# Finishing the last pair tile by tile: plain products for its output stage and its last two layers, buffers in places of x, and its heads placed closer together in the queue

## The chip, the cores and the metric

The kernel runs on one core of one Trainium2 chip. The metric is the device time of one execution in microseconds (us); lower is better. Engines are named as in the profile: PE (TensorE, matrix products; PEld is its weight load), DVE (VectorE), ACT (ScalarE), POOL (GpSimd) and SP (SyncE, which issues nearly all DMA transfers of this kernel).

## The reference, cut to what matters

The input x has 128 graphs of 64 nodes with 512 features. One adjacency matrix of 64x64 serves all graphs. Four layers follow one another; each adds its result to x and normalizes every row (layernorm without scale).

```python
x = _layernorm(x + L0(x))   # deg * (x Wi^T + b) + adj (x Wj^T)
x = _layernorm(x + L1(x))   # 4 attention heads + elu, output attention + elu, FFN, layernorm
x = _layernorm(x + L2(x))   # one graph attention head, product with W2
x = _layernorm(x + L3(x))   # the same with W3

def L1(x):
    h = elu(heads(x))                      # 4 heads of 512 -> 2048 features per row
    o = elu(attention(h @ W_out))          # one output head
    y = relu(o @ w1 + b1) @ w2 + b2 + o
    return layernorm(y) * gamma + beta

def L2(x):                                 # L3 alike
    Wh = x @ W
    logits = leaky_relu(Wh @ a_src + (Wh @ a_dst)^T, 0.2), masked by adj
    return softmax(logits) @ Wh
```

Everything is float32. The attention of one graph mixes only that graph's 64 rows, so two graphs of 64 rows make a tile of 128 rows that depends on no other tile.

## The kernel before, in words

The 8192 rows are cut into 32 pairs (NP), each of T = 2 tiles of P = 128 rows. A pair passes through five stages, each a Python generator: `stage_first` (layer 0), `stage_scores` (attention of the four heads, and the attention product with x), `stage_heads` (the heads' weight products, one generator for all pairs), `stage_project` (product with W_out into the tile `who`, in two halves q = 0 and 1, and the output attention's dots), and `stage_late`. That last one runs `stage_out` (output attention, elu, FFN, norms) and then `stage_gat` twice (layers 2 and 3). The FFN's second product and the products with W2 and W3 are Strassen-like: `strassen` and `seven` compute both tiles of a pair at once by 7 products in place of 8. Each product goes into one of two PSUM tiles (stx and sty in the profile), sums of operands are made on POOL, and DVE adds each partial result. Normalization of the first tile follows product 4, that of the second product 6. The weights of these products come as parts from DRAM (ws, wk) for each pair. hidp is already a plain product.

Two orders matter. First, a queue `queue` decides in which order the generators are asked for their next steps: each `yield n` puts the stage n units later. A turn is TURN = 107.0 units; pair p's stages start at fixed positions such as TURN * (p + 1.42) for its late stage. `seven` yields a gap between products (TURN / H / 8 in the heads); `stage_project` pauses TURN / 2 - 14.0 between its halves. At most UNITS = 3 products of seven are open in that order. Second, each step gets its number in this order as its rank. The planner (`Plan.order`) then simulates the engines with its own costs: on each engine the ready step of the lowest rank goes next. The result is the fixed instruction order of each engine. `soon()` lowers a step's rank; `together()` keeps calls in one step.

Buffers have tags with a number of places: x has 5 (one per pair in flight), who and o 1 each, A, rows, ys, s2 and s3 2 each, hT 4 (one per head), ax 1, PSUM 8 banks. A step that opens a tile waits until a place is free; the planner gives places within a reach of 160 steps (NEAR). `rows` loads one or two 512-element rows, broadcast over 128 partitions, into the rows tag.

At the end of the program the last pair but one (NP - 2) and the last (NP - 1) have start positions, paces and rests of their own:

```python
at, pace, rest = {NP - 2: (1.6, 1.0, 10.0), NP - 1: (1.3, 0.6, 0.0)}.get(
    p, (1.42, 1.0, 5.0)
)
start(TURN * (p + at), 10 * p, stage_late(p, pace, rest))
```

`pace` multiplies the late stage's yields, `rest` is added ahead of each of layers 2 and 3.

Of the kernel before, what the change touches and what calls it, by code (L numbers as in the profile page):

```python
# [12 lines left out]
FP = mybir.dt.float32  # L13
# [326 lines left out]
def gnn_stack_kernel(  # L340
# [347 lines left out]
    def moments(x, name):  # L688

        stats = small.tile([P, 6], FP, tag="stats", name=f"st_{name}")  # L690
        mv = small.tile([P, 2], FP, tag="mv", name=f"mv_{name}")
        nc.vector.bn_stats(stats, x)
        nc.vector.bn_aggr(mv, stats)
        rstd = small.tile([P, 1], FP, tag="rstd", name=f"rs_{name}")
        nc.gpsimd.tensor_scalar(rstd, mv[:, 1:2], EPS, None, ALU.add)
        nc.gpsimd.tensor_tensor(rstd, rstd, mhalf, ALU.pow)
        return mv[:, 0:1], rstd

    def normalize(x, name):

        mean, rstd = moments(x, name)
        shift = small.tile([P, 1], FP, tag="shift", name=f"sh_{name}")
        nc.vector.scalar_tensor_tensor(shift, mean, -1.0, rstd, ALU.mult, ALU.mult)
        nc.scalar.activation(x, x, AF.Identity, bias=shift, scale=rstd)
# [52 lines left out]
                nc.scalar.copy(aT[ts(b, N), :, s, :], pt[ts(s, N), :, ts(b, N)])  # L757
        return aT

    def attention(f, alpha, mask, fill, has, name):  # L760

        bc3 = [P, T, N]
        ps = psum.tile([P, T, P], FP, tag="b", name=f"bc_{name}")
        with nc.together():
            for t in range(T):
                nc.tensor.transpose(ps[:, t, :], f[:, 1, t : t + 1].to_broadcast([P, P]), ident)
        e = unit.tile(bc3, FP, tag="e1", bufs=2, name=f"e_{name}")
        with nc.soon():
            for b in range(2):
                nc.vector.tensor_tensor(  # L770
                    e[ts(b, N), :, :], ps[ts(b, N), :, ts(b, N)],
                    f[ts(b, N), 0, :].unsqueeze(2).to_broadcast([N, T, N]), ALU.add,
                )
# [19 lines left out]
        pt = psum.tile([P, P], FP, tag="b", name=f"pt_{name}")  # L793
        nc.tensor.transpose(pt, e.rearrange("p t j -> p (t j)"), ident)
        return pt

    def elu(dst, ps):

# [141 lines left out]
    def stage_heads():  # L940

        for i in range(NP * H):
            p, h = divmod(i, H)
            while p not in ys:
                yield 1.0
            y, t1, t2 = ys[p][h // 2]
            y, t1, t2 = y[:, :, h % 2, :, :], t1[:, :, h % 2, :], t2[:, :, h % 2, :]
            Y = lambda k, t: y[:, 2 * k : 2 * k + 2, t, :]
            w = w_h[h]
            hT = unit.tile([P, KC, T, P], FP, tag="hT", bufs=H, name=f"hT_{p}_{h}")  # L950

# [12 lines left out]
            def t4():  # L964
                nc.gpsimd.tensor_tensor(Y(1, 0), Y(1, 0), t2, ALU.subtract)

            yield from seven(
                product, lambda i, j: hT[:, 2 * i : 2 * i + 2, j, :], [2, P], f"h_{p}_{h}",
                TURN / H / 8, True,
                t4,  # L970
                lambda i: elu_of(hT[:, 2 * i : 2 * i + 2, :, :], f"{p}_{h}_{i}"),
            )
            hTs[p, h] = hT
            if h == H - 1:
                ys.pop(p)

    def stage_project(p):

        who = unit.tile([P, T, D], FP, tag="who", name=f"who_{p}")
        for q in range(H // 2):  # L980
            while (p, 2 * q + 1) not in hTs:
                yield 1.0
            h = [hTs.pop((p, 2 * q + k)) for k in range(2)]
            A = lambda k, t: h[k][:, :, t, :]
            nc.gpsimd.tensor_tensor(A(0, 1), A(0, 1), A(1, 1), ALU.add)
            yield from strassen(
                A, part_from(f"wo{q}", p), sums(A, KC, nc.gpsimd), who, KC, f"o_{p}_{q}", 3.0,
                fresh=q == 0,
            )
            if q == 0:  # L990
                yield TURN / 2 - 14.0
        r = rows([a_out[ts(s, D)] for s in range(2)], f"1o_{p}")
        yield 4.0
        f = small.tile([P, 2, T], FP, tag="f1", name=f"f_1o_{p}")
        dots(lambda s, t: f[:, s, t : t + 1], who, r, f"1o_{p}")
        outs[p] = (who, f)
        yield 0.0

    def stage_out(p):

        while p not in outs:
            yield 1.0
        x = xs[p]
# [9 lines left out]
        yield 2.0  # L1013
        o = unit.tile([P, T, D], FP, tag="o", name=f"o_{p}")
        oT = unit.tile([P, KC, T * P], FP, tag="A", bufs=NA, name=f"oT_{p}")

# [36 lines left out]
            yield 6.0  # L1053
        gamma_sb = rows([gamma], f"gamma_{p}")[:, 0, :]

        def norms(t):
            ot, xt = o[:, t, :], x[:, t, :]
            mean, rstd = moments(ot, f"1i_{p}_{t}")
            ps = psum.tile([P, D], FP, tag="b", name=f"ng_{p}_{t}")
            with nc.soon():  # L1060
                nc.vector.scalar_tensor_tensor(ps, ot, mean, gamma_sb, ALU.subtract, ALU.mult)
                nc.vector.scalar_tensor_tensor(xt, ps, rstd, xt, ALU.mult, ALU.add)
            normalize(xt, f"1_{p}_{t}")

        A = lambda k, t: hid[:, k, t, :, :]
        nc.gpsimd.tensor_tensor(A(0, 1), A(0, 1), A(1, 1), ALU.add)
        yield from strassen(
            A, part_from("w2", p, D // 2), sums(A, KC // 2, nc.gpsimd), o, KC // 2, f"y_{p}", 1.8,
            whole=norms,
        )  # L1070
        yield 4.0

    def stage_gat(p, name):
# [48 lines left out]
        if name == "3":  # L1122
            xs.pop(p)

    def stage_late(p, pace, rest):

        for later in stage_out(p):
            yield later * pace
        for name in ("2", "3"):
            yield rest  # L1130
            for later in stage_gat(p, name):
                yield later * pace


    queue = []

    def start(at, order, stage):
        heapq.heappush(queue, (at, order, stage))

    for p in range(NP):  # L1140
        if p < AHEAD:
            start(TURN * (0.2 * p - 1.2), 10 * p + 4, stage_first(p))
        else:
            start(TURN * (p - 1.1), 10 * p + 4, stage_first(p))
        start(TURN * (p - 0.5), 10 * p + 3, stage_scores(p))
        start(TURN * (p + 0.6), 10 * p + 2, stage_project(p))

        at, pace, rest = {NP - 2: (1.6, 1.0, 10.0), NP - 1: (1.3, 0.6, 0.0)}.get(
            p, (1.42, 1.0, 5.0)
        )  # L1150
        start(TURN * (p + at), 10 * p, stage_late(p, pace, rest))
    start(0.0, 10 * NP, stage_heads())
    start(-1.15 * TURN, 0, score_weights(
        [head_rows(w) for w in w_h], a_h, "h", lambda h: head_sums(w_h[h])
# [67 lines left out]
```

## Time and profile before

| | |
|---|---|
| median of 3 runs | 3366.57 us (3366.22 to 3369.87) |
| the profiled execution | 3368.96 us, its span 3367.2 us, mean granted clock of PE 0.989 |
| PE busy over the span | 98%; PEld 86%, DVE 73%, ACT 40%, POOL 51% |
| last product of the last pair's projection starts | 3257.45 us |
| last write of x by ACT | 3363.1 us |
| DMA over the span | 720 MB, 214 GB/s |

All instructions have the line L306 of a helper, so they are told apart by their tiles. In the names, ws_W is a part of W2 or W3, ws_w one of w2, ws_wo one of W_out; stx and sty with no suffix belong to layers 2 and 3 (and layer 0), with _o to the projection, with _y to the FFN, with _h to the heads. bc and pt are an attention's two transposes (with _1o those of the output attention), op its product, gp the attention product of layers 2 and 3. j and f are the dots with score rows. A float32 matmul is shown as two instructions, called halves below. Buffer numbers are left out, so the trace doesn't say which pair an instruction belongs to; that follows from order and dependences.

### The profile page before, as it was taken

The numbers are of one execution on the slowest core, as the hardware profiler recorded it, in microseconds if no ns is written. First come the engines' busy times: TensorE is split into PE (matmuls) and PEld (weight loads), VectorE is DVE, ScalarE is ACT, GpSimd is POOL, SyncE is SP. The second block draws the span as 40 slices with busy tenths as digits, with TensorE's granted clock in tenths as the row PEclk, the third lists the DMA queues.
The fourth block names the chain that finished last, engine by engine and source line by source line (L and its number), as shares of the span: only waits on it lengthen the run. The fifth ranks groups of instructions, "written<-read, shape, count | busy, mean of one in ns | idle before, by whom it ended". The sixth has DMA issues, their size and how long they took to land. (4 is left out here: it accounts for less than half of the span.)

```text
span 3367.2 us, 59757 instructions
## 1 busy us (share of the span) xinstructions
PE 3287.4 (98%) x21300; PEld 2901.8 (86%) x21300; DVE 2448.8 (73%) x5696; ACT 1354.8 (40%) x3180; POOL 1719.0 (51%) x1866
## 2 busy tenths in 40 slices
PE   8899999999999999999999999999999999999986
PEld 4788988888988988988888988988988888989974
DVE  6757777777777777777777777777767777777755
ACT  1344444444444343444443443443444433443432
POOL 6854455554455554455554455554455554555433
PEclk9899999999999999999999999999999999999997
DMA  8766667666666666666666666666666666666653
GB/s 285 260 218 207 206 215 223 215 222 217 207 205 230 217 218 220 213 207 222 216 217 224 205 214 217 216 216 229 202 216 214 221 211 225 198 222 210 205 162 112
DMA packets 302501, 720.43 MB, mean 214 GB/s; under 512 B 32848, under 2 KB 42112, under 8 KB 302208
## 3 DMA queue, kind: packets, MB, share of 16 engines
q1 hardware_dynamic: 302208, 716.63, 65.0%
q8 instruction: 171, 2.80, 0.3%
q14 instruction: 122, 1.00, 0.1%
HBM read 683.18 MB, written 33.32 MB: 213 GB/s over the span
## 5 line engine op out<-in xcount | busy, mean ns | idle before, releaser
L306 DVE CUSTOM_DVE_ANT_0 j<-x,rows 128x512 bf16<-128x512 f32 x736 | 616.7, 838 | 67.8 <-ACT x L306 35.7
L306 PE MATMUL stx_h<-ys,wh 128*128 128x128 f32 x3072 | 405.9, 276 | 0.9 <-ACT hT L306 0.5
L306 PEld LDWEIGHTS stx_h<-ys,wh 128*128 128x128 f32 x3072 | 387.1, 192 | 21.1 <-issue 9.2
L306 ACT COPY hT<-stx_h 128x256 f32<-128x256 f32 x384 | 143.0, 372 | 506.6 <-PE stx_h L306 497.2
L306 POOL TENSOR_SCALAR rs<-mv 128x1 f32<-128x1 f32 x256 | 85.4, 334 | 402.1 <-DVE mv L306 389.9
L306 ACT ACTIVATE x<-x,sh,rs 128x512 f32<-128x512 f32 x256 | 207.5, 814 | 201.1 <-DVE sh L306 199.2
L306 PE MATMUL sty_h<-ys,wh 128*128 128x128 f32 x2048 | 276.0, 278 | 0.6 <-ACT hT L306 0.6
L306 DVE TENSOR_TENSOR x<-stx,x 128x256 f32<-128x256 f32 x368 | 153.5, 419 | 158.0 <-PE stx L306 156.9
L306 PEld LDWEIGHTS sty_h<-ys,wh 128*128 128x128 f32 x2048 | 253.1, 193 | 13.3 <-issue 5.7
L306 PE MATMUL sty_o<-ws_wo,hT 128*128 128x256 f32 x1024 | 244.2, 381 | 1.7 <-DMA ws_wo<-d_wo 1.7
L306 PE MATMUL stx_o<-ws_wo_T,s_o 128*128 128x256 f32 x1024 | 244.6, 382 | 0.5 <-DVE who L306 0.3
L306 POOL TENSOR_TENSOR ys<-ys,t 128x256 f32<-128x256 f32 x128 | 113.2, 887 | 254.3 <-PE sty_h L306 254.2
L306 PE MATMUL hidp<-oT,w 128*128 128x256 f32 x1024 | 231.5, 379 | 0.7 <-ACT oT L306 0.7
L306 DVE TENSOR_TENSOR hT<-sty_h,hT 128x256 f32<-128x256 f32 x256 | 107.9, 421 | 165.9 <-PE sty_h L306 138.9
L306 PEld LDWEIGHTS hidp<-oT,w 128*128 128x128 f32 x1024 | 191.7, 190 | 25.2 <-ACT oT L306 0.9
L306 PEld LDWEIGHTS sty_o<-ws_wo,hT 128*128 128x128 f32 x1024 | 188.7, 190 | 26.6 <-issue 1.9
L306 PEld LDWEIGHTS stx_o<-ws_wo_T,s_o 128*128 128x128 f32 x1024 | 185.9, 190 | 25.6 <-DVE who L306 2.6
L306 ACT ACTIVATE elu<-hT 128x512 f32<-128x512 f32 x256 | 153.4, 601 | 102.8 <-DVE hT L306 91.4
L306 DVE SCALAR_TENSOR_TENSOR hT<-elu,hT 128x512 f32<-128x512 f32 x256 | 173.0, 682 | 28.7 <-ACT elu L306 26.0
L306 DVE BATCH_NORM_STATS2 st<-x 128x6 f32<-128x512 f32 x256 | 176.4, 689 | 5.5
L306 POOL TENSOR_TENSOR rs<-rs,mhalf 128x1 f32<-128x1 f32 x256 | 153.8, 601 | 21.3
L306 ACT COPY ys<-yp 128x512 f32<-128x512 f32 x256 | 131.3, 605 | 78.9 <-PE yp L306 73.2
(187 smaller groups left out, 7730.6 us busy)
## 6 DMA issues: line engine op xcount, KB each, us to landing
ws_wo_T<-d_wo_T SPq DMA_DIRECT2D x256, 512.0 KB, 3.9
ws_wo<-d_wo SPq DMA_DIRECT2D x192, 512.0 KB, 3.5
ws_W_T<-d_W_T SPq DMA_DIRECT2D x256, 256.0 KB, 3.6
rows<-d_h SPq DMA_DIRECT2D x240, 256.0 KB, 4.2
ws_w_T<-d_w_T SPq DMA_DIRECT2D x112, 512.0 KB, 4.2
ws_W<-d_W SPq DMA_DIRECT2D x192, 256.0 KB, 3.6
ws_w<-d_w SPq DMA_DIRECT2D x84, 512.0 KB, 4.2
ws_w_T<-d_w_T SPq DMA_DIRECT2D x128, 256.0 KB, 4.4
```

The costliest lines, as they stand in the source:

```text
L306: getattr(getattr(self.tc.nc, s.engine), name)(*map(real, args), **{k: real(v) for k, v in kw.items()})
```

## The change

Only the last pair and the one before it are scheduled or computed differently. For pair NP - 1, `stage_late` is replaced by `stage_last` (loads the whole of w2, W2, W3 and rows for b2 and gamma once, does the output attention for both tiles, loads the score rows of layers 2 and 3) and one `stage_tile` for each tile, which does elu, FFN, norms and both layers for 128 rows with plain products of 128x512. The heads' gaps and the projection's pause of that pair are multiplied by 0.6. Its `who` and `o` take places of the x tag, the whole weights those of ax and ys, the rows of b2 and gamma one of hT. The late stage of pair NP - 2 starts at 2.0 in place of 1.6, with pace 0.8 and no rest. `attention` gets T as an argument, `norms` becomes a function of its own, and the attention part of `stage_out` becomes `out_attention`.

```diff
-                TURN / H / 8, True,
+                TURN / H / 8 * haste(p), True,
...
-        who = unit.tile([P, T, D], FP, tag="who", name=f"who_{p}")
+        pool, tag = (unit, "who") if p < NP - 1 else (xp, "x")
+        who = pool.tile([P, T, D], FP, tag=tag, name=f"who_{p}")
...
-                yield TURN / 2 - 14.0
+                yield (TURN / 2 - 14.0) * haste(p)
...
+    def stage_last(p):
+        raw = {}
+        for name, src, tag, bufs in (("w2", w2, "ax", 1), ("W2", W2, "ys", 2), ("W3", W3, "ys", 2)):
+            raw[name] = unit.tile([P, KC, D], FP, tag=tag, bufs=bufs, name=f"{name}_last")
+            nc.sync.dma_start(out=raw[name], in_=src.rearrange("(c p) o -> p c o", p=P))
+        r = unit.tile([P, 2, D], FP, tag="hT", bufs=H, name="rows_last")
+        for i, src in enumerate((b2, gamma)):
+            nc.sync.dma_start(out=r[:, i, :], in_=src.partition_broadcast(P))
+        who, aT = yield from out_attention(p)
+        o = xp.tile([P, T, D], FP, tag="x", name=f"o_{p}")
+        shared.update(raw=raw, rows=r, who=who, aT=aT, o=o)
+        yield 2.0
+        for name in ("2", "3"):
+            shared[name] = rows([score[name][s, :] for s in range(2)], f"{name}_{p}")
+            yield 2.0
+
+    def stage_tile(p, t):
+        while "3" not in shared:
+            yield 1.0
+        x, o, r, raw = xs[p][:, t, :], shared["o"][:, t, :], shared["rows"], shared["raw"]
+        who, aT = shared["who"], shared["aT"]
+        def plain(lhsT, w, into, name):
+            ps = psum.tile([P, D], FP, tag="b", name=name)
+            for k in range(KC):
+                nc.tensor.matmul(ps, lhsT=lhsT(k), rhs=w[:, k, :], start=(k == 0), stop=(k == KC - 1))
+            nc.vector.tensor_tensor(into, ps, into, ALU.add)
+        ps = psum.tile([P, D], FP, tag="b", name=f"op_{p}_{t}")
+        with nc.together():
+            for b in range(2):
+                nc.tensor.matmul(
+                    ps[ts(b, N), :], lhsT=aT[ts(t, N), b, :], rhs=who[ts(t, N), b, :],
+                    start=True, stop=True)
+        elu(o, ps)
+        yield 3.0
+        both = unit.tile([P, 2, KC, P], FP, tag="A", bufs=NA, name=f"oT_{p}_{t}")
+        oT, hid = both[:, 0, :, :], both[:, 1, :, :]
...
+        nc.scalar.copy(oT, ps)
+        nc.gpsimd.tensor_tensor(o, o, r[:, 0, :], ALU.add)
+        yield 3.0
...
+        yield 4.0
+        plain(lambda k: hid[:, k, :], raw["w2"], o, f"yp_{p}_{t}")
+        norms(o, x, r[:, 1, :], f"{p}_{t}")
+        yield 8.0
+        for name in ("2", "3"):
+            f = small.tile([P, 2], FP, tag="f1", name=f"f_{name}_{p}_{t}")
...
+            pt = yield from attention(
+                f.unsqueeze(2), 0.2, mask2, never.to_broadcast([P, N]), has, f"{name}_{p}_{t}", 1)
+            aT = unit.tile([P, P], FP, tag="s3", bufs=2, name=f"aT_{name}_{p}_{t}")
+            nc.gpsimd.memset(aT, 0.0)
+            for b in range(2):
+                nc.scalar.copy(aT[ts(b, N), ts(b, N)], pt[:, ts(b, N)])
+            yield 2.0
+            gT = unit.tile([P, KC, P], FP, tag="s2", bufs=2, name=f"gT{name}_{p}_{t}")
+            ps = psum.tile([P, KC, P], FP, tag="b", name=f"gp{name}_{p}_{t}")
...
+            nc.scalar.copy(gT, ps)
+            yield 3.0
+            plain(lambda k: gT[:, k, :], raw[f"W{name}"], x, f"z{name}_{p}_{t}")
+            normalize(x, f"{name}_{p}_{t}")
+            yield 6.0
+        nc.sync.dma_start(out=out[ts(p * T + t, P), :], in_=x)
...
+    haste = lambda p: 0.6 if p == NP - 1 else 1.0
...
-        at, pace, rest = {NP - 2: (1.6, 1.0, 10.0), NP - 1: (1.3, 0.6, 0.0)}.get(
+        at, pace, rest = {NP - 2: (2.0, 0.8, 0.0), NP - 1: (1.3, 0.6, 0.0)}.get(
             p, (1.42, 1.0, 5.0)
         )
-        start(TURN * (p + at), 10 * p, stage_late(p, pace, rest))
+        if p < NP - 1:
+            start(TURN * (p + at), 10 * p, stage_late(p, pace, rest))
+        else:
+            start(TURN * (p + at), 10 * p, stage_last(p))
+            for t in range(T):
+                start(TURN * (p + at), 10 * p + 1 + t, stage_tile(p, t))
```

More of the change, by code (lines that the diff above doesn't have):

```diff
@@ L758, in attention_heads, with attention @@
         return aT
-    def attention(f, alpha, mask, fill, has, name):
+    def attention(f, alpha, mask, fill, has, name, T=T):
         bc3 = [P, T, N]
@@ L791, in attention, with norms @@
         yield 8.0
-        pt = psum.tile([P, P], FP, tag="b", name=f"pt_{name}")
+        pt = psum.tile([T * N, P], FP, tag="b", name=f"pt_{name}")
         nc.tensor.transpose(pt, e.rearrange("p t j -> p (t j)"), ident)
         return pt
+    def norms(o, x, gamma_sb, name):
+        mean, rstd = moments(o, f"1i_{name}")
+        ps = psum.tile([P, D], FP, tag="b", name=f"ng_{name}")
+        with nc.soon():
+            nc.vector.scalar_tensor_tensor(ps, o, mean, gamma_sb, ALU.subtract, ALU.mult)
+            nc.vector.scalar_tensor_tensor(x, ps, rstd, x, ALU.mult, ALU.add)
+        normalize(x, f"1_{name}")
     def elu(dst, ps):
@@ L997, in stage_project, with out_attention @@
         yield 0.0
-    def stage_out(p):
+    def out_attention(p):
         while p not in outs:
             yield 1.0
-        x = xs[p]
         who, f = outs.pop(p)
@@ L1013, in stage_out @@
         yield 2.0
+        return who, aT
+    def stage_out(p):
+        x = xs[p]
+        who, aT = yield from out_attention(p)
         o = unit.tile([P, T, D], FP, tag="o", name=f"o_{p}")
@@ L1054, in stage_out @@
         gamma_sb = rows([gamma], f"gamma_{p}")[:, 0, :]
[L1056 to L1063, printed above, removed]
         A = lambda k, t: hid[:, k, t, :, :]
@@ L1068, in stage_out @@
             A, part_from("w2", p, D // 2), sums(A, KC // 2, nc.gpsimd), o, KC // 2, f"y_{p}", 1.8,
-            whole=norms,
+            whole=lambda t: norms(o[:, t, :], x[:, t, :], gamma_sb, f"{p}_{t}"),
         )
@@ L1123, in stage_gat @@
             xs.pop(p)
+    shared = {}
+    def stage_last(p):
[6 more added lines that the diff above has]
+            nc.sync.dma_start(out=r[:, i, :], in_=src.partition_broadcast(P))
+        who, aT = yield from out_attention(p)
+        o = xp.tile([P, T, D], FP, tag="x", name=f"o_{p}")
[4 more added lines that the diff above has]
+            yield 2.0
@@ new lines, in stage_tile @@
+    def stage_tile(p, t):
[7 more added lines that the diff above has]
+                nc.tensor.matmul(
+                    ps, lhsT=lhsT(k), rhs=w[:, k, :], start=(k == 0), stop=(k == KC - 1)
+                )
+            nc.vector.tensor_tensor(into, ps, into, ALU.add)
+        ps = psum.tile([P, D], FP, tag="b", name=f"op_{p}_{t}")
+        with nc.together():
+            for b in range(2):
+                nc.tensor.matmul(
+                    ps[ts(b, N), :], lhsT=aT[ts(t, N), b, :], rhs=who[ts(t, N), b, :],
+                    start=True, stop=True,
+                )
+        elu(o, ps)
+        yield 3.0
+        both = unit.tile([P, 2, KC, P], FP, tag="A", bufs=NA, name=f"oT_{p}_{t}")
+        oT, hid = both[:, 0, :, :], both[:, 1, :, :]
+        ps = psum.tile([P, KC, P], FP, tag="b", name=f"oTp_{p}_{t}")
+        with nc.together():
+            for k in range(KC):
+                nc.tensor.transpose(ps[:, k, :], o[:, ts(k, P)], ident)
+        nc.scalar.copy(oT, ps)
+        nc.gpsimd.tensor_tensor(o, o, r[:, 0, :], ALU.add)
+        yield 3.0
+        ps = psum.tile([P, KC, P], FP, tag="b", name=f"hidp_{p}_{t}")
+        for c in range(KC):
+            with nc.together():
+                for k in range(KC):
+                    nc.tensor.matmul(
+                        ps[:, c, :], lhsT=w1_sb[:, k, ts(c, P)], rhs=oT[:, k, :],
+                        start=(k == 0), stop=(k == KC - 1),
+                    )
+        for c in range(KC):
+            nc.scalar.activation(
+                hid[:, c, :], ps[:, c, :], AF.Relu, bias=b1_sb[:, c : c + 1]
+            )
+        yield 4.0
[4 more added lines that the diff above has]
+            f = small.tile([P, 2], FP, tag="f1", name=f"f_{name}_{p}_{t}")
+            for s in range(2):
+                junk = unit.tile([P, D], BF, tag="junk", name=f"j_{name}_{p}_{t}_{s}")
+                nc.vector.tensor_tensor_reduce(
+                    junk, x, shared[name][:, s, :], 1.0, 0.0, ALU.mult, ALU.add,
+                    accum_out=f[:, s : s + 1],
+                )
+            yield 2.0
+            pt = yield from attention(
+                f.unsqueeze(2), 0.2, mask2, never.to_broadcast([P, N]), has, f"{name}_{p}_{t}", 1
+            )
+            aT = unit.tile([P, P], FP, tag="s3", bufs=2, name=f"aT_{name}_{p}_{t}")
+            nc.gpsimd.memset(aT, 0.0)
+            for b in range(2):
+                nc.scalar.copy(aT[ts(b, N), ts(b, N)], pt[:, ts(b, N)])
+            yield 2.0
+            gT = unit.tile([P, KC, P], FP, tag="s2", bufs=2, name=f"gT{name}_{p}_{t}")
+            ps = psum.tile([P, KC, P], FP, tag="b", name=f"gp{name}_{p}_{t}")
+            with nc.together():
+                for c in range(KC):
+                    nc.tensor.matmul(
+                        ps[:, c, :], lhsT=x[:, ts(c, P)], rhs=aT, start=True, stop=True
+                    )
+            nc.scalar.copy(gT, ps)
[4 more added lines that the diff above has]
+        nc.sync.dma_start(out=out[ts(p * T + t, P), :], in_=x)
```

## The prediction, made before the result was known

> **What bounds the kernel now.** I read the page's slices first, then the busy time by stretch, then TensorE's timeline and the chain of waits at the end. The slices (tenths busy, then granted clock) show a full TensorE everywhere but at both ends:
>
> ```profile
> PE   8899999999999999999999999999999999999986
> PEclk9899999999999999999999999999999999999997
> ```
>
> By stretch the columns are: stretch, length, then busy us (and instructions) of PE, PEld, DVE, ACT, POOL, then clock, DMA share, GB/s:
>
> ```profile
> 3000.00:3100.00 100.00, 100.00 (x655) 89.15 (x654) 71.57 (x173) 40.48 (x93) 49.40 (x56) 1.00 0.64 208
> 3200.00:3261.70 61.70, 59.27 (x326) 51.89 (x324) 35.98 (x84) 20.25 (x50) 23.62 (x31) 1.00 0.59 187
> ...
> 3279.40:3312.30 32.90, 26.18 (x117) 20.17 (x116) 22.33 (x55) 10.88 (x24) 13.93 (x20) 0.90 0.52 159
> 3312.30:3339.70 27.40, 17.17 (x67) 13.35 (x67) 13.39 (x36) 4.98 (x13) 7.70 (x12) 0.79 0.41 132
> 3339.70:3367.20 27.50, 13.49 (x50) 10.36 (x50) 10.44 (x30) 4.89 (x14) 4.43 (x9) 0.69 0.15 51
> 3261.70:3367.20 105.50, 65.89 (x267) 50.88 (x267) 57.42 (x156) 25.62 (x69) 29.62 (x44) 0.77 0.34 106
> ```
>
> Until 3259 TensorE sets the pace: only less work ahead of that point could help. From 3261.7, where DVE has added the last product of the last pair (31) into `who`, to the end, 105.5 us, no engine is full: PE 62%, DVE 54%. That tail is a chain of latencies; in it lie pair 30's layers 2 and 3 and all of pair 31 behind `who`. Its milestones on TensorE's timeline (start, length, instruction, idle before):
>
> ```profile
> 3257.45 1.99 PE L306 MATMUL stx_o<-ws_wo_T,hT 128*128 128x256 f32 x8 [0.17 <-DVE who L306]
> ...
> 3279.40 1.09 PE L306 MATMUL op<-who,aT_1o 64*64 64x512 f32 x8
> ...
> 3285.71 3.72 PE L306 MATMUL hidp<-oT,w 128*128 128x256 f32 x16 [0.68 <-ACT oT L306]
> ...
> 3319.18 3.79 PE L306 MATMUL gp<-aTg,x 128*128 128x128 f32 x16 [0.74 <-ACT aTg L306]
> ...
> 3347.70 3.78 PE L306 MATMUL gp<-aTg,x 128*128 128x128 f32 x16 [1.22 <-ACT aTg L306]
> ```
>
> In pair 31: 17.7 us from `who` to its output attention's product (op), 32.9 to its normalized x (3312.3), 27.4 for layer 2 (to 3339.7), 24.2 for layer 3 (to 3363.9), 3.3 to the end; sum 105.5. The chain of waits names a weight load and seven products in a fixed order:
>
> ```profile
> 3326.55 3.67 DMA ws_W_T<-d_W_T
> ...
> 3357.23 2.13 issue
> ```
>
> **What the Trainium skill says.** "TensorE: Matmul & The Clock Gate", section "What's actually happening": the array runs at half clock after an idle window of about 3.4 us, and at full clock after as long a busy one. The trace agrees: 16 halves of gp take 1.95 us at 3228.5, inside the full stretch, and 3.78 at 3347.7 in the tail. "VectorE: DVE Perf Modes", section "The TRN2 errata": an fp32 tensor_tensor of N elements takes (N+151)/0.96 ns. The trace agrees (290 ns for N = 128 against 292 measured; 691 for 512 against 692), so I use it for N = 64, which no row shows: 224 ns, an estimate.
>
> **The change, part by part** (positions below are in the queue's own turns; a step that is ready and has the lower position goes first; they are no times).
>
> 1. *Where `who` of pair 31 ends.* The heads' gap times 0.6 ends their positions 0.4 turn earlier (31.6, not 32.0); the pause in `stage_project` falls from 39.5 to 23.7, so the second half of the projection lies at 32.04 to 32.27, not 32.19 to 32.42. Pair 30's late stage goes from 31.6 to 32.0. TensorE is full there, so only the order counts: what is moved behind `who` brings it forward. Pair 30's output stage holds on PE: op 1.0, oTp 0.9, hidp 32 halves by 0.216 = 6.9, y 7 products by 0.865 = 6.05, small transposes 0.3; 15.2 in all, all ahead of 3257.5 now. Its Strassen product (32.25 to 32.38) surely goes behind, the rest partly, as ready steps fill gaps. Bounds 0 and 15.2; I take y and one of the two hidp groups, 6.05 + 3.45 = **9.5**: `who` at 3252.2. At nothing I cost `who` and `o` in places of x: no later pair loads an x.
>
> 2. *From `who` to op* (17.7 now). Now four dots are mixed with pair 30's, then attention, and a rows load that was issued at 3259.9. Floor: two dots behind the last add 2 by 0.73 = 1.5, then 4.9 (bc at 3314.26 to gp at 3319.18 is the same chain) = 6.5. Pair 30's adds and norms of y (9.6 us on DVE) now lie here; I take **11**, 6.7 less.
>
> 3. *Output stage by tile* (32.9 now). op 0.6; elu 0.6 + 0.63 + 0.67 + 0.1 = 2.0; oTp and copy 0.63 + 0.04 + 0.59 = 1.3; hidp 16 products of 128 columns by 0.216 = 3.5, last Relu 0.3; w2 plain: 4 products of 512 columns by 0.86 = 3.5; drain and one add 0.9; both norms from the chain's rows 6.8. Sum 18.9. The second tile trails by about its share of PE or DVE, 4.5: **23.4**, 9.5 less. Gone: three POOL sums on the path (0.88, 1.06, 0.73) and the wait for seven products.
>
> 4. *Layers 2 and 3 by tile* (27.4 + 24.2 = 51.6 now). Two dots 1.5; attention 4.9 less five DVE steps by 0.067, one exponential (0.35) and two of four copies (0.42), = 3.8; gp 8 halves, 0.9 warm to 1.9 cold, 1.4; gT copy 0.7; plain product 3.5; drain and add 0.9; normalize 0.70 + 0.19 + 0.63 + 1.0 + 0.17 + 0.82 and gaps = 3.7. Sum 15.5, twice **31**, 20.6 less. Three plain products cost 16 pieces where Strassen has 14, +0.865 us of PE each, 2.6 in all: within the 3.5s.
>
> 5. *What is added beside it.* DMA: 21 part loads of 256 KB go, three weights of 1 MB and the same rows come, five issues by some 0.3 us on SP. A 512 KB load lands in 3.5 to 4.2 us, so 1 MB in some 7.5; w2's place (ax) is free long before, those of W2 and W3 (ys) after pair 31's heads, over 30 us before use. POOL clears a 128x128 tile four times by 0.20 while attention runs, and adds b2 (1.3) under hidp; cover gone, that is 2 us. Attention's transposed tile of 64 rows instead of 128, and one DVE gT sum less, count nothing.
>
> Sum for pair 31: 11 + 23.4 + 31 + 3.3 = 68.7 with the engines free. They are not: DVE has some 35 us of pair 31 and 31 of pair 30 (y 9.6, layers 2 and 3 some 11 each) to do. I add 9 for steps queued behind pair 30's, 4 for cold starts of PE in 18 us of products, 2 for SP, which issues in order. 3252.2 + 83.7 = 3335.9.
>
> 6. *Pair 30* is late next. Its late stage is the old form: pair 31 took 102.2 us for it, `who` to last x. At position 32.0 it comes after heads (24.5 of PE), half the projection (12.1) and pair 29's rest (18), all from 3176.1 where the heads begin: 3231 at the latest by order. 3231 + 102.2 + 3.3 = 3336.5, before it meets the tiles. Two chains that end together: I add 2.5, **span 3338.4, 29 less than 3367.2**. The profiled execution took 3368.96, 1.8 beyond its span; the runs' median 3366.57 is 2.4 below that. 3366.6 - 29 = **3338**.
>
> **The rivals.** *Pair 30's layer 3 is last.* `rows` has two buffers, and the shared rows of layers 2 and 3 hold both; pair 30's own layer 3 row must wait until both tiles' dots of layer 2 are done, about 11 + 23.4 + 9 = 43 after `who`. Then landing 3.9, layer 27.4, some 10 to 20 of interference, 3.3: 3252.2 + 88 to 98 = 3340 to 3350; later still if 3's row is freed last (15 more). Median 3344 to 3357. For it: gT of the old layer waits on DMA and order now. Against: tiles do their dots early.
>
> *Slower: the old chain of pair 30 starts too late.* If its output attention starts only when `who` of pair 31 is done (the planner fills with heads and projection until then), it ends at 3252.2 + 102.2 + 15 of interference + 3.3 = 3372.7, 5.5 over: median 3372. It decides at a start of 3246.7. Against: its inputs are ready about 3190, and now its first transpose (bc_1o) runs at 3202.
>
> *It doesn't do what it says:* heads cannot run faster than their inputs and elu allow, `who` stays at 3261.7, and DVE's queue eats the tiles' gain: within 0.2%.
>
> **Numbers.** About 0.2% (6.7 us) is what a measurement of this kernel can tell from no change. Likeliest case 0.66, at 3338 (3318 to 3350: `who` at 3246.5 and 6 of queueing instead of 15 gives 3320; nothing gained before `who` gives 3348). Pair 30 last 0.20. Slower 0.09, 3373 to 3380. No effect 0.05. Faster 0.66 + 0.20 = 0.86. The range 3318 to 3360 leaves out slower, no effect and about 0.06 of the others.
>
> **What would show it.** Right: the last stx_o at 3245 to 3253; the tail about 85 us with DVE near 75%; no stx of pair 31 behind its `who`, but z products of 128x512; op at 8 to 14 us behind `who`; steps of a tile's layer 15 to 20 us. Wrong: a last output row from pair 30 long after the tiles'; SP waiting on rows over 5 us with W3 parts queued behind; PE idle before `who`; first bc_1o of pair 30 behind 3245.

## The result, and the profile after

The changed kernel takes **3351.09 us** (median of 6 runs, 3349.53 to 3354.35) where the kernel before takes 3367.12 (6 runs beside it): ratio **0.9951 [0.9938, 0.9964]**, 16 us faster. The forecast was 3338 (3318 to 3360), with 3318 to 3350 for its likeliest case: the sign was right, the gain a little over half of the 29 us expected, and just outside that likeliest case.  The profiled execution took 3351.91 us with a span of 3350.1, 17.1 less than before.

The slices of the page (tenths busy, tenths of granted clock):

```profile
PE   8899999999999999999999999999999999999997
PEclk9999999999999999999999999999999999999998
```

Only the end tells: the last two digits of PE are 9 and 7 where they were 8 and 6, and the last of the clock is 8 where it was 7. The busy time by stretch says more. Columns as before; the last row is the tail, from the end of `who` to the end of the span:

```profile
3200.00:3241.70 41.70, 38.87 (x205) 33.10 (x204) 21.53 (x55) 14.62 (x38) 13.18 (x14) 0.96 0.71 228
3241.70:3262.60 20.90, 20.40 (x99) 16.90 (x97) 12.34 (x33) 5.15 (x16) 7.48 (x12) 1.00 0.60 185
3262.60:3293.40 30.80, 24.37 (x132) 17.35 (x132) 23.55 (x58) 12.09 (x29) 13.64 (x21) 0.94 0.28 81
3293.40:3319.00 25.60, 17.05 (x55) 10.20 (x53) 14.91 (x50) 5.76 (x14) 5.05 (x11) 0.83 0.27 81
3319.00:3345.00 26.00, 20.05 (x81) 14.36 (x81) 15.21 (x48) 7.65 (x24) 4.54 (x9) 0.83 0.09 32
3241.70:3350.10 108.40, 81.88 (x365) 58.81 (x363) 66.18 (x188) 31.50 (x82) 31.48 (x55) 0.88 0.29 90
```

**The tail did not get shorter; it starts earlier.** `who` ends at 3241.7, 20.0 us before its old place (3261.7), and the tail takes 108.4 us, 2.9 more than its old 105.5. It holds 81.88 us of PE, 16.0 more than before; PE stands idle in it for 108.4 - 81.9 = 26.5 us, 13.1 less than before (39.6). So the tail took in 16 us of products that used to lie ahead of `who`, and paid with 2.9 us of length. The forecast had it the other way round: `who` 9.5 earlier and a tail some 19 shorter. Over the whole span PE is busy for 3284.4 us in place of 3287.4, so 3.0 of the 17.1 us are less busy time of PE, and 14.1 are less idle time.

The milestones of pair 31 on TensorE's timeline:

```profile
3224.40 3.11 PE L306 MATMUL sty_o<-ws_wo,hT 128*128 128x256 f32 x8 [2.83 <-DMA ws_wo<-d_wo]
...
3239.22 1.99 PE L306 MATMUL stx_o<-ws_wo_T,hT 128*128 128x256 f32 x8
...
3253.20 1.89 PE L306 MATMUL hidp<-oT,w 128*128 128x256 f32 x8
3254.92 0.38 PE L306 MATMUL bc_1o<-ident,f_1o 128*128 128x128 f32 x2
...
3262.61 1.09 PE L306 MATMUL op<-who,aT_1o 64*64 64x512 f32 x8
...
3268.18 7.31 PE L306 MATMUL hidp<-oT,w 128*128 128x128 f32 x64
3275.33 3.60 PE L306 MATMUL yp<-w_last,oT 128*128 128x512 f32 x8
```

No hidp of pair 30 is left ahead of 3239.22: all four groups of 8 run behind it, the last at 3253.20, and its FFN products behind them. Pair 31's output attention, whose dots DVE has finished at 3245.6, gets its first transpose (bc_1o) only behind that last group, 9.3 us later. The order on PE is fixed, so a transpose of 0.38 us waits for all of it.

The first of these lines (3224.40) holds a new wait. A part of W_out comes 8.9 us after its issue, where the median for such a part is 3.6 to 3.9 us on the page. It is issued behind one of the whole weights and two broadcast rows, and the DMA engines have no room: from 3210 to 3225 their busy share is 0.99, with 320 GB/s, where it was 0.54 with 175 GB/s in the same stretch before.

```profile
3210.28 0.38 SPq L306 DMA_DIRECT2D W_last<-in_W_dram  x1
...
3212.30 0.97 SPq L306 DMA_DIRECT2D rows_last<-in_b_dram  x1
3213.32 0.76 SPq L306 DMA_DIRECT2D rows_last<-in_gamma_dram  x1
...
3215.43 1.96 SPq L306 DMA_DIRECT2D ws_wo<-d_wo  x2
```

PE stands for 2.83 us, and this product and the next run slow (3.11 and 2.50 us in place of 1.89). That is about 4.7 us ahead of `who` which the prediction costed at nothing. That the big loads delay the part is read from their order, the DMA share and the landing time; e7 and e3, below, bear on it.

The end, in ACT's writes of x (the last four):

```profile
3336.23 0.81 ACT L306 ACTIVATE x<-x,sh,rs 128x512 f32<-128x512 f32 x1 [2.79 <-DVE sh L306]
3340.77 0.81 ACT L306 ACTIVATE x<-x,sh,rs 128x512 f32<-128x512 f32 x1 [3.73 <-DVE sh L306]
3344.22 0.81 ACT L306 ACTIVATE x<-x,sh,rs 128x512 f32<-128x512 f32 x1 [2.64 <-DVE sh L306]
3346.18 0.81 ACT L306 ACTIVATE x<-x,sh,rs 128x512 f32<-128x512 f32 x1 [1.15 <-DVE sh L306]
```

The second and third are pair 31's tiles; the first and the last are pair 30's. Both pairs end within 2 us.

### The profile page after: what moved, and what is told of

Read it like the earlier page. It is cut to its first block, busy times and chain, and to the rows that moved or that the text cites. A ratio compares the mean times of both kernels' runs of the same rounds, so it can differ in the third digit from the quotient of the medians.

```text
span 3350.1 us, 59710 instructions
## 1 busy us (share of the span) xinstructions
PE 3284.4 (98%) x21298; PEld 2891.1 (86%) x21298; DVE 2432.1 (73%) x5698; ACT 1356.2 (40%) x3184; POOL 1714.0 (51%) x1860
## 3 DMA queue, kind: packets, MB, share of 16 engines
q14 instruction: 124, 1.02, 0.1%
## 4 chain that ended last, share of the span: by engine, by line
PE 92%; DMA 3%; DVE 3%; issue 1%; SPq 1%; POOL 1%; ACT 0%; POOLq 0%; DVEq 0%
PE stx_h L306 13%; PE stx_o L306 13%; PE stx L306 12%; PE sty_h L306 10%; PE sty_o L306 10%; PE sty L306 9%; PE hidp L306 6%; PE yp L306 4%; PE gp L306 3%; PE stx_y L306 3%; PE sty_y L306 2%; PE axp L306 2%; PE bc L306 1%; PE op L306 1%; PE oTp L306 1%
## 5 line engine op out<-in xcount | busy, mean ns | idle before, releaser
L306 PE MATMUL hidp<-oT,w 128*128 128x256 f32 (+1 forms) x1056 | 231.8, 373 | 0.0
```

The source lines that it names most:

```text
L306: getattr(getattr(self.tc.nc, s.engine), name)(*map(real, args), **{k: real(v) for k, v in kw.items()})
```

## The experiments

Three parts can be told apart, each a bundle that is not split further here: **H**, the heads' and the projection's 0.6; **L**, the later and quicker start of pair 30's late stage; **T**, the tile form with its whole weights and buffers. My theory after the result: H and L bring `who` forward by ordering work behind it, T makes room for that work by shortening pair 31's chain, and neither is worth much alone. The rivals: one part carries the gain by itself (H through an earlier `who`, or T through a shorter tail); or a wait in the tail, for rows or for a transfer, holds the end and hides the rest.

### The parts, alone and in twos

H is undone by `haste = lambda p: 1.0`, L by the old entry of the table, T by the old call:

```diff
-    haste = lambda p: 0.6 if p == NP - 1 else 1.0
+    haste = lambda p: 1.0                                   # no H
...
-        at, pace, rest = {NP - 2: (2.0, 0.8, 0.0), NP - 1: (1.3, 0.6, 0.0)}.get(
+        at, pace, rest = {NP - 2: (1.6, 1.0, 10.0), NP - 1: (1.3, 0.6, 0.0)}.get(   # no L
...
-        if p < NP - 1:
-            start(TURN * (p + at), 10 * p, stage_late(p, pace, rest))
-        else:
-            start(TURN * (p + at), 10 * p, stage_last(p))
-            for t in range(T):
-                start(TURN * (p + at), 10 * p + 1 + t, stage_tile(p, t))
+        start(TURN * (p + at), 10 * p, stage_late(p, pace, rest))                  # no T
```

e1_haste is H alone:

> Only the quicker pace of the last pair's heads and projection (haste 0.6), with that pair's who in a place of x; late stages of pairs 30 and 31 as before. Order theory (the gain comes from work moved behind the last pair's projection): half of the order part is here, 3 to 8 us faster than before, who of pair 31 about 5 to 10 us earlier than 3261.7 and a tail longer by part of it. Tile theory (the gain comes from the shorter chain of a tile): within 3 us of before.

e2_late30 is L alone:

> Only pair 30's late stage put later (2.0, pace 0.8, no rest), with pair 31's who in a place of x; heads and pair 31's late stage as before. Order theory: 3 to 10 us faster, because pair 30's output stage goes behind who of pair 31 and fills idle time of the tail. Rival (the old form of pair 30's late stage is too long to begin so late): 0 to 8 us slower, its layer 3 ending last.

e3_order is H and L:

> Haste and pair 30's later start together, who of pair 31 in a place of x, but no tiles: pair 31 keeps its old late stage with products of seven. Order theory: most of the 16 us are here, 9 to 16 us faster than before. Tile theory: 0 to 6 us faster, and without tiles the tail behind who is over 115 us.

e4_tiles is T alone:

> Only the tile-by-tile late stage of pair 31 (with its loads and places); no haste, pair 30's late stage as before. Tile theory (as in the prediction): who at 3261.7 as before, tail shorter by 15 to 22 us, so 15 to 22 us faster than before. Order theory: the tail is filled by queueing behind pair 30's work on DVE and PE, 0 to 8 us faster.

e5_nohaste is L and T:

> The changed kernel without haste (heads and projection of the last pair at the old pace). If haste is what brings who forward, who ends 10 to 16 us later than 3241.7 and the time is 4 to 8 us above the changed kernel's 3351. If heads run as soon as their inputs allow anyway, within 2 us of it.

e6_old30 is H and T:

> The changed kernel with pair 30's late stage at its old start, pace and rest (1.6, 1.0, 10.0). If pair 30's work is the filler that makes the earlier who worth something, who ends 6 to 12 us later than 3241.7 and the time is 4 to 10 us above 3351. If pair 30's late stage now lies in the tiles' way (its dots, attention and gp ahead of theirs), the time is 3 to 10 us below 3351.

Measured, each against the kernel before on the same chip. The tail runs from the end of `who` to the end of the span; its idle time is its length less PE's busy time in that stretch.

| parts | ratio [95%] | `who` ends | op of pair 31 | tail, us | PE busy / idle in it |
|---|---|---|---|---|---|
| none (before) | 1 | 3261.7 | 3279.4 | 105.5 | 65.9 / 39.6 |
| H (e1) | 1.0022 [1.0015, 1.0028] | 3255.1 | 3285.0 | 118.4 | 67.3 / 51.2 |
| L (e2) | 1.0020 [1.0011, 1.0029] | 3257.5 | 3273.2 | 117.1 | 65.5 / 51.6 |
| T (e4) | 0.9990 [0.9984, 0.9997] | 3254.9 | 3283.3 | 108.0 | 67.2 / 40.8 |
| H, L (e3) | 0.9979 [0.9969, 0.9989] | 3236.3 | 3253.0 | 121.1 | 81.4 / 39.7 |
| L, T (e5) | 0.9986 [0.9979, 0.9992] | 3257.9 | 3274.2 | 106.3 | 70.6 / 35.7 |
| H, T (e6) | 0.9997 [0.9988, 1.0005] | 3251.9 | 3283.0 | 110.9 | 68.4 / 42.5 |
| H, L, T (after) | 0.9951 [0.9938, 0.9964] | 3241.7 | 3262.6 | 108.4 | 81.9 / 26.5 |

What follows:

- **H and L are worth something only together.** Each alone costs about 7 us (0.0022 and 0.0020 of 3368); both save 7 (0.0021). Their sum would be a loss of 14. In the traces `who` comes 4 to 7 us earlier with one and 25.4 with both. The timeline of TensorE in e2 shows why L alone does little:

```profile
3240.50 7.07 PE L306 MATMUL hidp<-oT,w 128*128 128x256 f32 x32
...
3250.00 1.03 PE L306 MATMUL stx_y<-ws_w,hid 128*128 128x256 f32 x4
3250.86 1.03 PE L306 MATMUL sty_y<-ws_w,hid 128*128 128x256 f32 x4
...
3255.18 1.03 PE L306 MATMUL stx_o<-ws_wo_T,hT 128*128 128x256 f32 x4
```

  All 32 hidp halves of pair 30 and its first FFN products still run ahead of the last stx_o (the row shows its first four halves): the projection keeps its old, later place in the queue, and ready work of pair 30 goes ahead of it. With H alone the last group of the heads' products starts at 3211.5 in place of 3233.8, but pair 30 keeps its old rank ahead of the projection. In e3, as in the changed kernel, every hidp and FFN product of pair 30 runs behind the last product of `who`.
- **T shortens the tail beside the other parts, and not alone.** Beside H, L or both it takes 7.5, 10.8 and 12.7 us from the tail; alone it takes none (108.0 against 105.5), `who` comes 6.8 earlier, and 0.1% is left.
- **Idle time falls much only with all three.** With H and L the tail is 15.6 us longer, about the 15.5 us of PE that it takes in, and its idle time stays (39.7 against 39.6): of the 9.8 us that the span of e3 loses, 6.3 are PE's busy time over the whole span (3281.1 against 3287.4 us, with the same 21300 instructions). With T as well, 26.5 us of idle time are left.
- What T adds to H and L, 0.9979 to 0.9951 (some 9 us), is more than what it gives alone (3.4 us); the 6 us between the two are only about as large as their own uncertainty.

No part alone gains more than 3.4 us, and no two together more than some 7 of the 16: that rules out a single carrier.

The expectations missed this. e1 and e2 were expected to be 3 to 8 and 3 to 10 us faster by the theory of order, and both came 7 slower; e3 fell between its two theories (7 us faster, with a tail of 121.1); e4 met the one of queueing; e5 and e6 lie some 12 and 15 us above the changed kernel, where at most 8 and 10 were expected. Only the rival of e2 had a part that loses alone.

### Why haste alone costs: two places of `rows`

The traces of e1, e4 and e6 showed `who` ready and its dots late. Two rows of e1's timeline:

```profile
3264.78 0.81 SPq L306 DMA_DIRECT2D rows_1o<-in_a_out_dram  x2
...
3268.95 0.69 DVE L306 CUSTOM_DVE_ANT_0 j_1o<-who,rows_1o 128x512 bf16<-128x512 f32 x1
```

and of the changed kernel's:

```profile
3230.25 0.86 SPq L306 DMA_DIRECT2D rows_1o<-in_a_out_dram  x2
...
3240.52 0.33 SPq L306 DMA_DIRECT2D rows_gamma<-in_gamma_dram  x1
3241.59 0.68 DVE L306 CUSTOM_DVE_ANT_0 j_1o<-who,rows_1o 128x512 bf16<-128x512 f32 x1
```

In e1 `who` ends at 3255.1 and its score rows are issued at 3264.78. With pair 30 at its old start, its own rows for the norm and for layer 2 come first in the order and hold both places of the rows tag. With L the order is reversed: rows_1o at 3230.25, gamma of pair 30 at 3240.52, and the dots begin as `who` ends. e10_haste_place is e1 with rows_1o of pair 31 in one of the heads' places, e9_old30_place is e6 with the same edit:

```diff
-        r = rows([a_out[ts(s, D)] for s in range(2)], f"1o_{p}")
+        if p < NP - 1:
+            r = rows([a_out[ts(s, D)] for s in range(2)], f"1o_{p}")
+        else:
+            r = unit.tile([P, 2, D], FP, tag="hT", bufs=H, name=f"rows_1o_{p}")
+            for s in range(2):
+                nc.sync.dma_start(out=r[:, s, :], in_=a_out[ts(s, D)].partition_broadcast(P))
```

> e1_haste (haste alone, 3376, 7 us slower than before) with the same edit: the two rows for pair 31's output attention in a place of hT. There who ended at 3255.1, the rows were issued at 3264.8 and the first dot began at 3268.9. Rows theory: first dot within 1 us of who, 8 to 13 us below 3376, so at or below before. Rival (haste alone takes the filler from the tail): less than 3 us below 3376.

Two rows of its timeline:

```profile
3215.74 0.86 SPq L306 DMA_DIRECT2D rows_1o<-in_a_out_dram  x2
...
3256.05 0.68 DVE L306 CUSTOM_DVE_ANT_0 j_1o<-who,rows_1o 128x512 bf16<-128x512 f32 x1
```

The ratio goes from 1.0022 to **1.0000 [0.9992, 1.0009]** and op from 3285.04 to 3274.80. So the wait for a place of `rows` is the loss of haste alone. It hid no gain: without the wait, a `who` that is 5.6 us earlier than before buys nothing.

> e6_old30 (haste and tiles, pair 30's late stage at its old start) with one edit: pair 31's two rows for the output attention's dots get a place of hT in place of one of rows. In e6 who of pair 31 ended at 3251.9, but the rows were issued only at 3262.1, when pair 30's gamma gave up its place, and the first dot began at 3265.7. Rows theory (the two places of rows couple pair 31's dots to pair 30's norms, and the later start of pair 30 only helps because it turns their order round): first dot within 1 us of who, and 8 to 13 us below e6's 3368. Rival (pair 30's late work is simply in the way on PE and DVE): less than 3 us below.

Here op comes 12.5 us earlier (3270.44 against 3282.98) and the ratio goes from 0.9997 only to 0.9989 [0.9982, 0.9995]; the intervals of the two overlap, and under 3 us was what the rival expected. So this wait is not what separates e6 from the changed kernel (0.9951). Why L alone costs 7 us was not isolated: op comes 6.2 earlier than before, and still the last layer of pair 31 ends last, some 8 us later (last write of x at 3370.83 against 3363.09). The rival of e2 had the size right (0 to 8 us slower), but it expected pair 30's layer 3 to end last.

### Waits in the changed kernel that might hold the end

e7_loads issues the whole weights and the rows of b2 and gamma behind the output attention in the order of steps, to free SP ahead of the projection:

```diff
     def stage_last(p):
+        who, aT = yield from out_attention(p)
         raw = {}
         for name, src, tag, bufs in (...):
...
-        who, aT = yield from out_attention(p)
```

> The changed kernel with the loads of w2, W2, W3 and the rows of b2 and gamma placed after the output attention in the order of steps, so that they do not go ahead of the last projection parts. In the changed kernel PE waited 2.83 us for a part of W_out at 3224.4 that took 8.9 us to land, then ran two products at half clock (5.6 us in place of 3.8). If those 3.2 MB are the cause: no such wait, who 3 to 5 us earlier, 3 to 5 us below 3351. If the time is set by what comes later: who earlier but within 1.5 us of 3351. If the weights come late for the tiles: slower.

0.9950 [0.9938, 0.9963], but the experiment didn't do what it was meant to: SP issued W_last at 3211.61, 1.3 us later than before the edit, presumably because these steps wait for nothing but a place, and the wait for ws_wo stayed at 2.60 us. e3, which leaves out T and with it the whole weights, says more. There the product that waits in the changed kernel runs without a wait:

```profile
3218.79 1.89 PE L306 MATMUL sty_o<-ws_wo,hT 128*128 128x256 f32 x8
```

The DMA share from 3210 to 3225 is 0.83 there, ws_wo's parts land in 4.5 us at most, and `who` ends at 3236.3, 5.4 us earlier than in the changed kernel. So the wait comes with T, and takes back part of what T saves in the tail. That the loads alone cause it is not shown, since e3 leaves out all of T. With T but without H (e5) ws_wo's parts land in 4.4 us at most. With H and T (e6) one takes 9.0 us too, but PE has products of pair 30 to run and doesn't wait. Fewer bytes there (W3 into ax once w2 is used) were not tried.

e8_rows takes the prediction's first rival, that pair 30's layer 3 waits for its row. The score rows shared by the two tiles go to the heads' places:

```diff
-            shared[name] = rows([score[name][s, :] for s in range(2)], f"{name}_{p}")
+            r = unit.tile([P, 2, D], FP, tag="hT", bufs=H, name=f"rows_{name}_last")
+            for s in range(2):
+                nc.sync.dma_start(out=r[:, s, :], in_=score[name][s, :].partition_broadcast(P))
+            shared[name] = r
```

> The changed kernel with the tiles' shared score rows of layers 2 and 3 in free places of hT, so the two places of rows are left to pair 30. If pair 30's layer 3 waits for these places (the rival of the prediction), its dots come earlier and the time falls by 3 to 8 us below 3351. If not, within 2 us.

0.9952 [0.9940, 0.9965]. The wait for a place was there: in the changed kernel pair 30's layer 3 rows are issued at 3295.47, just behind the tiles' dots of layer 2, while in e8 the last rows are issued by 3272.1. But it held nothing up: the rows land in some 4.3 us, about 3300, and the first dot that uses them runs at 3311.24. Freeing the place changes nothing, so the rival's mechanism is out, though its time (3344 to 3357) was met.

e11_urgent gives every step of `stage_last` and `stage_tile` a rank lower by 2000 (the cut shows `stage_last` alone), so that wherever it is ready it goes ahead of pair 30:

```diff
-            s = Step(engine, len(self.steps) - self.early)
+            s = Step(engine, len(self.steps) - self.early - self.base)
...
+    def urgent(stage):
+        while True:
+            nc.base = 2 * SOON
+            later = next(stage, None)
+            nc.base = 0
...
-            start(TURN * (p + at), 10 * p, stage_last(p))
+            start(TURN * (p + at), 10 * p, urgent(stage_last(p)))
```

> The changed kernel with all steps of stage_last and stage_tile of pair 31 at the head of each engine's choice (their rank lowered by 2000). In the changed kernel the tail behind who is 108.4 us, where 83.7 were predicted; bc_1o waited 9.3 us on PE behind pair 30's hidp and pair 29's layer 3. If queueing behind the older pairs is what fills the tail: bc_1o within 2 us of its dots, pair 31's outputs 10 to 20 us earlier, and 4 to 10 us below 3351 (pair 30 then ends last). If the sum of work, not its order, sets the end: within 3 us of 3351. If pair 30's chain is the bound: 3 to 12 us above.

0.9952 [0.9940, 0.9965]. op moves from 3262.6 to 3253.3, and of the last four writes of x the first two are now the tiles' (L307 is the same helper):

```profile
3327.54 0.80 ACT L307 ACTIVATE x<-x,sh,rs 128x512 f32<-128x512 f32 x1
3331.33 0.81 ACT L307 ACTIVATE x<-x,sh,rs 128x512 f32<-128x512 f32 x1 [1.55 <-DVE sh L307]
3340.26 0.81 ACT L307 ACTIVATE x<-x,sh,rs 128x512 f32<-128x512 f32 x1 [7.23 <-DVE sh L307]
3344.34 0.81 ACT L307 ACTIVATE x<-x,sh,rs 128x512 f32<-128x512 f32 x1 [3.27 <-DVE sh L307]
```

The tiles end 13 us earlier than in the changed kernel and pair 30 takes their place at the end. Priority alone decides who is last, not when.

e12_alone leaves out pair 30's layers 2 and 3:

```diff
     def stage_late(p, pace, rest):
...
+        if p == NP - 2:
+            for t in range(T):
+                nc.sync.dma_start(out=out[ts(p * T + t, P), :], in_=xs[p][:, t, :])
+            return
```

> The changed kernel without pair 30's layers 2 and 3: pair 30's x is written out behind layer 1. This measures the tiles' own chain. If the prediction's prices for a tile's layers (15.5 us each) are right and only the meeting with pair 30's old chain made them 25 to 31 us, a tile layer takes 15 to 18 us here, and the span ends 18 to 25 us below 3350. If the prices were too low in themselves (cold PE, two tiles on one DVE), a layer takes 20 us or more and the span ends 5 to 14 us below 3350.

0.9911 [0.9897, 0.9924], which is 3338.27 us: 0.0040 of 3368, some 13 us below the changed kernel. That is what pair 30's two layers cost in the changed kernel's tail. The rest is the tiles' own chain and what still lies ahead of it in the tail, pair 29's layer 3 and pair 30's output stage:

```profile
3239.60:3333.40 93.80, 65.03 (x271) 43.22 (x270) 47.23 (x130) 23.59 (x58) 23.03 (x41) 0.85 0.17 53
3289.10:3309.30 20.20, 12.59 (x36) 6.71 (x36) 9.38 (x32) 4.39 (x12) 2.80 (x6) 0.75 0.00 0
3309.30:3330.50 21.20, 14.04 (x35) 7.60 (x35) 7.74 (x26) 4.39 (x12) 1.56 (x4) 0.70 0.03 12
```

Its two layers, with no work of pair 30 beside them, take 20.2 and 21.2 us at a granted clock of 0.75 and 0.70. I had put them at 15.5. TensorE in the last layer shows where it goes:

```profile
3307.95 0.29 PE L306 MATMUL bc<-ident,f 128*128 128x128 f32 x1 [3.19 <-DVE f L306]
...
3313.10 2.04 PE L306 MATMUL gp<-aT,x 128*128 128x128 f32 x8 [0.60 <-ACT aT L306]
...
3315.87 2.08 PE L306 MATMUL z<-W_last,gT 128*128 128x512 f32 x2 [0.52 <-ACT gT L306]
3317.74 1.92 PE L306 MATMUL gp<-aT,x 128*128 128x128 f32 x8
3319.45 7.37 PE L306 MATMUL z<-W_last,gT 128*128 128x512 f32 x14
```

The first tile's product z gets its first quarter at 3315.87, then stands behind the second tile's gp, and runs on from 3319.45. DVE adds it at 3323.42, 7.5 us after its start, where the product was priced at 3.5. The first two halves take 2.08 us where they take 1.02 at 3333.46 in the changed kernel: half clock, which the Trainium skill ("TensorE: Matmul & The Clock Gate", section "What's actually happening") gives TensorE after an idle window of about 3.4 us. Here two idle stretches of 3.19 and 3.22 us, with one transpose between them, lie ahead. From bc to gp it is 5.15 us, not 3.8. The attention and the way from z to its add make up most of the 5.7 us by which this layer exceeds its price.

## Why the prediction was right, and where its sum was off

| step | predicted, us | measured | in e12 |
|---|---|---|---|
| 1. `who` earlier by | 9.5 (0 to 15.2) | 20.0 | 22.1 |
| 2. `who` to op | 11 | 20.9 | 20.9 |
| 3. op to the second tile's x | 23.4 | 30.8 | 28.6 |
| 4. two layers | 31 | 51.6 | 41.4 |
| end | 3.3 | 5.1 | 2.9 |
| queueing, cold starts, SP, pair 30 | 17.5 | in the rows above | |

Measured tail: 20.9 + 30.8 + 51.6 + 5.1 = 108.4; predicted 86.2. The miss of 22.2 in the tail, less the 10.5 by which `who` came earlier than forecast, is the 11.7 us between the spans 3338.4 and 3350.1. That the time fell within the range is in part luck: two misses of opposite sign, each larger than 10 us, were set off against each other. The direction was argued rightly in step 1 (work moved behind `who` brings it forward), but the larger part of the forecast gain, a shorter tail, did not come. Of the five signs named for "right" only the z products appeared; the last stx_o (3239.22), the tail (108.4), op (20.9 behind `who`) and a tile's layers (25.6 and 26.0 us) all lie outside what was named. PE idle ahead of `who`, a sign for "wrong", did appear (2.83 us).

1. **`who`: the upper bound was broken.** Of the 20.0 us, 18.2 are the earlier start of its last product (3239.22 against 3257.45), the rest a quicker add on DVE. I had counted pair 30's output stage alone (15.2 us) as what can go behind. All its hidp and FFN went, and so did the layer 3 work of pair 29 (gp at 3241.05 and its seven products, about 8 us of PE), which I had not listed as movable. Against that stood the wait for ws_wo (some 4.7 us), costed at nothing in step 5. What can be moved behind a product is everything ready whose rank is near, not only the stage whose start is edited.
2. **`who` to op.** Right that the dots start at once (3241.59); wrong that DVE's adds for pair 30 set the pace. The dots are done 3.9 us after `who`, then bc_1o waits 9.3 us in PE's order behind the very work that step 1 moved. I counted that work as a gain in step 1 and not as a queue in step 2. e11 takes 6.6 us off this stretch (14.3) and gains nothing at the end.
3. **Output stage.** hidp of both tiles stands in one row (3268.18, 64 halves, 7.31 us), so the first tile's yp waits for the second tile's hidp. I had put 4.5 us of trailing at the end of the stage and nothing ahead of it. 28.6 in e12, without pair 30's layers.
4. **Two layers: the term that was mis-sized most.** The two layers take 51.6 us, just what they took before, so nothing of the 20.6 us forecast for them came. Some 10 of these are the tiles' own: e12 measures 41.4 without pair 30's layers. There one tile's product stands behind the other's on PE, and starts at half clock (the lines above), where the sum took each chain as free. The other 10 come from meeting pair 30's products, of which TensorE's timeline of the changed kernel shows the pattern:

```profile
3301.96 2.08 PE L306 MATMUL z<-W_last,gT 128*128 128x512 f32 x2 [0.81 <-ACT gT L306]
3303.83 1.91 PE L306 MATMUL stx<-ws_W_T,s 128*128 128x256 f32 x4
3305.53 1.78 PE L306 MATMUL gp<-aT,x 128*128 128x128 f32 x8
3307.15 1.88 PE L306 MATMUL z<-W_last,gT 128*128 128x512 f32 x4
3308.87 1.03 PE L306 MATMUL stx<-ws_W_T,gT 128*128 128x256 f32 x4
3309.74 4.45 PE L306 MATMUL z<-W_last,gT 128*128 128x512 f32 x10
```

   One tile's product is cut by two pieces of pair 30 and by the other tile's gp, each a DVE or ACT step late.
5. **Beside it.** The four memsets take 0.20 us each and lie off the path as said, the three 1 MB loads land in 6.3 to 7.0 us (7.5 forecast), and the estimate of 224 ns for N = 64 from the Trainium skill ("VectorE: DVE Perf Modes", section "The TRN2 errata") is met: 0.22 to 0.23 us for three of the four in the changed kernel, 0.53 for one. What these loads do to a neighbour was missed (step 1). PE's sum fell to 3284.4 us from 3287.4, so the 2.6 us more that the plain products were priced at don't show in it.
6. **Pair 30.** "Two chains that end together" held: its last write of x comes 2 us behind the tiles'. Its first bc_1o lies at 3216.9, ahead of the 3231 given as the latest. The 17.5 us added for queueing and for pair 30 are not far from what pair 30's layers cost (13 us, e12). What was too low is the sum under them: 68.7 us for pair 31's chain alone, where the tail of e12 takes 93.8.

The slower rival (pair 30's chain too late, decided at 3246.7) is out by 30 us, and "no effect" by the interval. DVE is 61% busy in the tail (66.18 of 108.4), not 75%, because the tail is longer, not because DVE did less.

What holds the end now is not one wait. Neither a free row (e8), nor first rank for the tiles (e11) moves the time; taking work out of the tail does (e12). How far it is the clock in PE's gaps and how far the chains' own steps was not separated.

## What to carry to other kernels

Where an engine runs full up to a critical product, bringing that product forward only orders other work behind it, and what follows decides whether that pays. So such edits must be priced, and tried, together: here each order edit alone lost 7 us, both gained 7, and with the tile form behind them 16; the idle time of the tail fell from 39.6 to 26.5 us only with all three. Price chains that share an engine with a fixed order as one queue, not as free chains with an addition on top: work counted as a gain ahead of a point comes back as a queue behind it, and two interleaved chains took 20 us a layer where the free sum said 15.5. And look for small shared buffers (here two places of `rows`): a stage moved in the order can find them held by a neighbour.

## What was not expected of the hardware

A 512 KB part issued 5.2 us behind a 1 MB load and two broadcast rows landed in 8.9 us, where its like takes 3.6 to 3.9 at the median; the DMA engines had a busy share of 0.99 from 3210 to 3225. TensorE's granted clock fell to 0.66 (3225 to 3230) after it stood for only 2.83 us, and its next eight halves took 3.11 us in place of 1.89. And the busy share of a stretch does not give its clock by itself: with TensorE busy for 62 and 66% of the time it was granted 0.75 and 0.70 (e12's two layers), with 67 and 77% 0.83 (the changed kernel's), and with 63% 0.79 in the kernel before (3312.3 to 3339.7).
